# A binary convolution layer: own input buffers for even and odd rows, sign passes ordered behind the chunks, and y added to unscaled rows

## The chip, the cores and the metric

The kernel runs on one core of a Trainium2 chip. The metric is the device time of one launch in microseconds; the time of a kernel is the median of several runs. Engines are named as in the profile: PE (TensorE, matrix multiplication), PEld (its weight loads), DVE (VectorE), ACT (ScalarE), POOL (GpSimd) and SP (SyncE). SP only issues transfers here, POOL issues those that add to what lies in memory, and ACT issues a few stores.

## The reference

The network has four residual layers on a float32 tensor of 4 images, 256 channels, 64 x 64 pixels: an axial attention, a ternary convolution, a binary convolution and a convolution with generated weights. Each computes x = x + layer(group norm of x). The change concerns the third, cut to its computation:

```python
def _L2_conv_ref(x, w1, w2, g1, b1, g2, b2, g3, b3):
    x = channel_shuffle(x, 2)
    xa, xb = jnp.split(x, 2, axis=1)
    x1 = jnp.sign(x)
    x1 = gconv3x3(x1, w1, stride=1, groups=2)
    x1 = leaky_relu(x1)                              # slope 0.01
    x2 = batchnorm_train(x1, g1, b1)
    x3 = jnp.concatenate((x2 + xa, xb), axis=1)
    x3 = batchnorm_train(x3, g2, b2)
    x3 = channel_shuffle(x3, 2)
    x4 = jnp.sign(x3)
    x4 = gconv3x3(x4, w2, stride=1, groups=2)
    x4 = leaky_relu(x4)
    x4 = batchnorm_train(x4, g3, b3)
    x5a, x5b = jnp.split(x3, 2, axis=1)
    return jnp.concatenate((x4 + x5a, x5b), axis=1)
# in the network:  x = x + _L2_conv_ref(_gn(x), ...)
```

batchnorm_train takes mean and variance over the batch and all pixels, so the second convolution cannot start before the first has run on all four images.

## The kernel before

The attention and the ternary layer come first, then the binary layer (from 1884 to 2224 us of the trace), then the last layer, whose names begin with g. A tile scheduler orders each engine's instructions at compile time and sets the semaphore waits; each engine then works through its list in order. `tc.issue_after(ins)` puts what is traced inside it behind `ins` in the list of that instruction's engine, and adds no semaphore; `tc.high_priority()` moves work forward.

The channels of an image are kept as 128 even (t = 0) and 128 odd ones (t = 1), after the shuffle. "Even rows" and "odd rows" are these. The image is cut into halves h of 32 pixel lines, loaded with one more line (33 x 64 = 2112 elements in each of 128 partitions, 1056 KB, line 1704). A half is two chunks q. In `binary_conv` a chunk is 72 bf16 matmuls (L1613): 18 into each of four PSUM tiles m0 to m3, of which there are seven buffers. It works on transformed rows: `binary_rows` makes four combinations (e_tr, L1602, DVE) of the signs in a padded tile (e_pad), and each pair of image lines then costs four products rather than six. The chunk is emptied by an ACT copy of m1 (L1621), four DVE additions (L1622 to L1625), two DVE steps with the leaky slope that write y and its sums (L1628), and an ACT Square that sums y squared (L1631).

Pass 1 (`prepare_1`, `chunk_1`): for each half and t the rows are loaded (SP), ACT takes the sign of the rows less their group mean (L1726), and DVE transforms. For odd rows ACT then also writes scale times row plus bias over the rows (L1719), and POOL adds them to the output in memory (`into_out`, L1712). The cross sum of y and the even rows (L1739) gives, with the sums, the statistics of y + xa. The next image's half is prepared in the program's text after chunks 1 and 3 of the current one (`images`). The five row buffers are taken in turn, three in pool xp3 and one each in xp1 and xp2, whatever the rows are. What frees a buffer is for even rows the sign and the cross sums, and for odd rows the landing of the accumulating transfer.

Between the passes a chain of small DVE steps (L1796 to L1820 in the text) and two ACT calls gives the batch norm's factors: `sx`, `cx` per image for the rows, `sy1`, `cy1` for y, and `sa`, their product.

Pass 2 (`prepare_2`, `chunk_2`): the odd rows are loaded again, and ACT's sign with scale and bias is taken in two groups of 64 partitions (L1831). The even rows are loaded, scaled by ACT in place over all 2112 elements (L1847), y times `sa` is added by DVE (L1851), and then comes the plain sign in two groups (L1831). DVE transforms, and POOL adds the finished even rows to the output. Two entries in `ahead` keep the halves in order. The first half of image 0 is prepared in two steps of 17 and 16 lines. After chunks 1 and 3, ACT issues a store of y (L1870).

The last layer is traced after it. Its early steps share engines with pass 2: loads of finished output rows (`fetch`, SP), two measuring passes on ACT (L1267, L1268) placed behind chunks (2,1) and (2,2), a small norm, memsets of its padded tile (L1231), which uses memory that held y, and its first transforms (L1073 to L1095) and matmuls (L1113).

Of the kernel before, what the change touches and what calls it, by code (L numbers as in the profile page):

```python
# [9 lines left out]
F32 = mybir.dt.float32  # L10
F32R = mybir.dt.float32r
BF16 = mybir.dt.bfloat16
AF = mybir.ActivationFunctionType
ALU = mybir.AluOpType
# [4 lines left out]
P = 128  # L19
B = 4  # L20
# [21 lines left out]
def network(ctx: ExitStack, tc, x, wqkv, relm, relt, relw, relv, counts, masks, vecs, rowv, ab, w1, l2w1, l2w2, l3w, mats, out):  # L42
# [4 lines left out]
    nc = tc.nc  # L47
# [3 lines left out]
    keep = ctx.enter_context(tc.tile_pool(name="keep", bufs=1))  # L51
# [46 lines left out]
    def small(pool, shape, base="sm"):  # L98
        name = fresh(base)
        return pool.tile(shape, F32, name=name, tag=name)  # L100
# [65 lines left out]
    with ExitStack() as ph:  # L166
        wp = pool(ph, "a_w")
        xp_ = pool(ph, "a_x", 6)
        sp = pool(ph, "a_s")
# [5 lines left out]
        psp = pool(ph, "a_ps", 2, PSUM)  # L175
# [37 lines left out]
        squares = []  # L213
# [554 lines left out]
    def from_scores(general, keep):  # L768
# [836 lines left out]
        def binary_conv(psp, lp, parts, vs, q, dst, sums, squares, name):  # L1605

            ms = []
            for k in range(4):
                m = psp.tile([P, 8, 64], F32, name=f"{name}_{k}", tag="conv")
                for i in range(3):  # L1610
                    for dx in range(3):
                        for g in range(2):
                            nc.tensor.matmul(  # L1613
                                m[64 * g : 64 * g + 64], lhsT=parts[:, g, i, k, dx, :],
                                rhs=vs[g][:, k, 8 * (q % 2) : 8 * (q % 2) + 8, dx : dx + 64],
                                start=(i == 0 and dx == 0), stop=(i == 2 and dx == 2), tile_position=(0, 64 * g),
                            )
                ms.append(m)
            o = lp.tile([P, 2, 8, 64], F32, name=f"{name}_o", tag="lk")
            t, c = o[:, 0], o[:, 1]  # L1620
            nc.scalar.copy(c, ms[1])  # L1621
            nc.vector.tensor_tensor(t, ms[2], c, ALU.add)  # L1622
            nc.vector.tensor_tensor(c, c, ms[2], ALU.subtract)
            nc.vector.tensor_tensor(t, ms[0], t, ALU.add)
            nc.vector.tensor_tensor(c, c, ms[3], ALU.subtract)  # L1625
            rows = dst.rearrange("p (q r w) -> p r q w", r=2, w=64)
            for r in range(2):
                nc.vector.scalar_tensor_tensor(  # L1628
                    rows[:, r], o[:, r], 0.01, o[:, r], ALU.mult, ALU.max, accum_out=sums[:, r : r + 1]
                )  # L1630
            return nc.scalar.activation(o.rearrange("p r q w -> p (r q w)"), dst, AF.Square, accum_out=squares).ins  # L1631

        with ExitStack() as ph:
# [51 lines left out]
            def inside(t, h, rows=slice(0, P)):  # L1685
                return pads[t][h][rows, 1 - h : 34 - h, 1:65]
# [7 lines left out]
                binary_rows(v, pads[t][h])  # L1694
                return v

            taken = [0]

            def rows_of(b, t, h, name):

                xt = (xp3, xp3, xp3, xp1, xp2)[taken[0] % 5].tile([P, 33, 64], F32, name=f"{name}_{b}_{t}_{h}", tag="x2")
                taken[0] += 1
                r = 31 * h
                nc.sync.dma_start(
                    out=xt.rearrange("p h w -> p (h w)"), in_=x2_d[b][bass.ts(t, P), r * 64 : (r + 33) * 64]
                )
                return xt

            xa, xb = {}, {}

            def into_out(b, h, odd, xt):
                nc.gpsimd.dma_start(  # L1712
                    out=out[b].rearrange("(p two) f -> two p f", two=2)[odd][:, bass.ts(h, HW // 2)],
                    in_=xt.rearrange("p h w -> p (h w)")[:, 64 * h : 64 * h + HW // 2], accum_op=ALU.add,
                )

            def add_odd(b, h):
                own = xb[b, h][:, h : h + 32]
                nc.scalar.activation(own, own, AF.Identity, bias=cx[:, 1, b : b + 1], scale=sx[:, 1, b : b + 1])  # L1719
                into_out(b, h, 1, xb[b, h])  # L1720

            def prepare_1(b, h):
                vs = []
                for t in range(2):
                    xt = rows_of(b, t, h, "x2")
                    nc.scalar.activation(inside(t, h), xt, AF.Sign, bias=ngm2[:, b, t : t + 1])  # L1726
                    vs.append(transformed(b, t, h, 0))
                    (xa, xb)[t][b, h] = xt
                if b > 0:
                    add_odd(b, h)  # L1730
                return vs

            def chunk_1(b, q, vs):
                dst = y[b][:, bass.ts(q, 1024)]
                binary_conv(psp, lp, parts[0], vs, q, dst, sums[0][:, b, q], squares[0][:, b, q : q + 1], f"pc1_{b}_{q}")
                h = q // 2
                r = 16 * (q % 2) + h
                junk = jp.tile([P, 1024], BF16, name=f"junk_{b}_{q}", tag="junk")
                nc.vector.scalar_tensor_tensor(  # L1739
                    junk, dst, 1.0, xa[b, h][:, r : r + 16, :].rearrange("p h w -> p (h w)"), ALU.mult, ALU.mult,  # L1740
                    accum_out=cross[:, b, q : q + 1],
                )
# [34 lines left out]
            def half_scales(t, shift):  # L1777
                sz, cz = bn_affine(
                    sp, mean[:, t : t + 1], var[:, t : t + 1], vec[:, V_G2 + t : V_G2 + t + 1],
                    vec[:, V_B2 + t : V_B2 + t + 1], 1,  # L1780
                )
                if shift is not None:
                    nc.vector.scalar_tensor_tensor(cz, shift, sz, cz, ALU.mult, ALU.add)
                nc.vector.tensor_scalar(sx[:, t], rs2[:, :, t], sz, None, ALU.mult)
                nc.vector.tensor_scalar(cx[:, t], nmr2[:, :, t], sz, cz, ALU.mult, ALU.add)
                return sz

            half_scales(1, None)
            for h in range(2):
                add_odd(0, h)  # L1790
            images(prepare_1, chunk_1, ready)
# [9 lines left out]
            w = small(sp, [P, B])  # L1801
            nc.vector.scalar_tensor_tensor(w, my, 1.0 / HW, nmr2[:, :, 0], ALU.mult, ALU.mult)
            nc.vector.tensor_tensor(e, e, w, ALU.add)
            cov = small(sp, [P, 1])
            nc.vector.tensor_reduce(cov, e, AX.X, ALU.add)
            w = small(sp, [P, 1])
# [5 lines left out]
            nc.vector.scalar_tensor_tensor(var[:, 0:1], w, sy1, var[:, 0:1], ALU.mult, ALU.add)  # L1812
            nc.vector.tensor_scalar(var[:, 0:1], var[:, 0:1], 0.0, None, ALU.max)
            nc.vector.tensor_tensor(mean[:, 0:1], mean[:, 0:1], vec[:, V_B1 : V_B1 + 1], ALU.add)
            sa = small(sp, [P, 1])
            nc.vector.tensor_tensor(sa, sy1, half_scales(0, cy1), ALU.mult)

# [1 line left out]

            def prepare_2(b, h):
                xts = [rows_of(b, t, h, "x3") for t in range(2)]

                def signs(t, rows):
                    for g in range(2):
                        kw = {} if t == 0 else {
                            "bias": cx[64 * g : 64 * g + 64, 1, b : b + 1],
                            "scale": sx[64 * g : 64 * g + 64, 1, b : b + 1],
                        }  # L1830
                        sign = nc.scalar.activation(  # L1831
                            inside(g, h, slice(64 * t, 64 * t + 64))[:, rows], xts[t][64 * g : 64 * g + 64, rows],
                            AF.Sign, **kw,
                        )
                    return sign

                signs(1, slice(0, 33))
                vs = [slot(b, g, h, 1) for g in range(2)]

                steps = ((0, 17, 0), (17, 33, 8)) if b == h == 0 else ((0, 33, 0),)  # L1840
                n = 16 // len(steps)
                with ExitStack() as order:
                    for i in ahead:
                        order.enter_context(tc.issue_after(i))
                    for r0, r1, pair in steps:
                        xt = xts[0][:, r0:r1]
                        nc.scalar.activation(  # L1847
                            xt, xt, AF.Identity, bias=cx[:, 0, b : b + 1], scale=sx[:, 0, b : b + 1]
                        )
                        xf = xt.rearrange("p h w -> p (h w)")  # L1850
                        nc.vector.scalar_tensor_tensor(  # L1851
                            xf, y[b][:, 64 * (31 * h + r0) : 64 * (31 * h + r1)], sa, xf, ALU.mult, ALU.add
                        )
                        sign = signs(0, slice(r0, r1))
                        for g in range(2):
                            row = binary_rows(vs[g], pads[g][h], pair, n)
                ahead[:] = [sign.ins, row.ins]
                into_out(b, h, 0, xts[0])
                return vs

            ends = {}

            def chunk_2(b, q, vs):
                ends[b, q] = binary_conv(
# [162 lines left out]
```

## Time and profile before

| what | value |
|---|---|
| time, median of 3 runs | 2702.37 us (2691.62 to 2704.37) |
| the profiled execution's own time | 2695.66 us |
| its span in the trace | 2693.9 us |
| granted PE clock, mean | 0.94 |
| binary layer in the trace | about 1884 to 2224 us |
| PE busy in its 2304 matmuls | 273.7 us |
| ACT's wait for rows at the pass-1 signs | 54.9 us in 8 waits |
| PE idle between the passes | 17.66 us |

A group line of the profile reads: line, engine, operation, output and input names with buffer numbers left out, shapes, count; then busy time in us and the mean of one in ns; then the engine's idle time just before these instructions, with what ended most of it. A wait line reads: engine, tile and line that waited, what it waited for, us in total, times (in the binary layer's answer also the longest). A timeline line has the start, the duration, and the instruction; idle time before it stands in brackets. A stage line has, for each engine, busy time and instructions, and then the PE clock, the DMA share and GB/s.

### The profile page before, as it was taken

What the parts mean: (1) busy time and instruction counts of PE and PEld (TensorE: products, weight loads), DVE (VectorE), ACT (ScalarE), POOL (GpSimd) and SP (SyncE); (2) the same over time, 40 slices, a digit from 0 to 9 for tenths busy, and PEclk for the clock granted to TensorE, in tenths of its full rate; (3) what the DMA queues carried; (4) which work ended last, traced back from release to release, by engine and by line L of the source; (5) the groups of instructions that cost most, each with busy time, mean ns of one, the idle gap of its engine ahead of it and who ended that gap; (6) DMA issues with size and microseconds to landing.
All of it is one profiled execution on the core that took longest, in us unless ns stands there. A gap on an engine that the chain in (4) does not pass through costs nothing. (4 is left out here: it accounts for less than half of the span.)

```text
span 2693.9 us, 78726 instructions
## 1 busy us (share of the span) xinstructions
PE 2323.6 (86%) x34816; PEld 1620.9 (60%) x34816; DVE 1977.6 (73%) x3326; ACT 1299.7 (48%) x2114; POOL 167.8 (6%) x285
## 2 busy tenths in 40 slices
PE   7999888888998788878884999998887887899998
PEld 4656655556666566667663777776444444566665
DVE  6766787888876466666667989986677787688884
ACT  3556354555555654454434655553445753433210
POOL 0000100000000100000000011111000010100000
PEclk9999899999999789989896999999988997999999
DMA  6866476667666887777777666525655775746221
GB/s 234 269 194 196 127 196 183 169 155 202 177 156 146 251 276 252 255 245 257 249 237 255 225 206 226 181 110 193 160 152 170 237 263 150 160 108 148 42 47 49
DMA packets 284832, 505.64 MB, mean 188 GB/s; under 512 B 32896, under 2 KB 149248, under 8 KB 270784
## 3 DMA queue, kind: packets, MB, share of 16 engines
q1 hardware_dynamic: 214336, 347.46, 42.3%
q0 software_dynamic: 21888, 94.32, 13.8%
q10 hardware_dynamic: 48256, 58.73, 6.2%
q8 instruction: 275, 4.51, 0.7%
q14 instruction: 77, 0.63, 0.1%
HBM read 270.45 MB, written 229.97 MB: 186 GB/s over the span
## 5 line engine op out<-in xcount | busy, mean ns | idle before, releaser
L515 DVE STREAM_TRANSPOSE t<-pd 128x1024 f32<-128x1024 f32 x256 | 304.4, 1227 | 84.0 <-PE pd L508 83.1
L508 PE MATMUL pd<-rm,qb 64*32 64x256 f32 x8192 | 310.7, 390 | 48.8 <-DVE t L515 34.6
L1613 PE MATMUL pc<-e_tr,e_k 128*64 128x512 bf16 x2304 | 273.7, 399 | 59.5 <-DVE e_tr L1602 27.9
L535 ACT ACTIVATE o<-pq 128x512 f32<-128x512 f32 x256 | 150.5, 593 | 280.6 <-PE pq L529 280.6
L1113 PE MATMUL gc<-gtr,g_u 128*128 128x512 f32 x576 | 262.6, 608 | 12.8 <-DVE gtr L1077 5.4
L1613 PEld LDWEIGHTS <-e_k 128*64 128x64 bf16 x2304 | 155.6, 114 | 175.6 <-issue 73.9
L508 PEld LDWEIGHTS pd<-rm,qb 64*32 64x32 f32 x8192 | 171.5, 108 | 143.9 <-DVE t L515 60.5
L1509 PE MATMUL dc<-dh,d_u 128*128 128x512 f32 x768 | 230.9, 412 | 23.8 <-ACT dh L1486 21.1
L940 ACT ACTIVATE pt<-pt,sm 128x512 f32<-128x512 f32 x256 | 162.3, 709 | 167.6 <-DVE pt L910 167.6
L1509 PE MATMUL dc<-dl,d_u 128*128 128x512 f32 x768 | 226.5, 405 | 0.9 <-DVE dl L1487 0.7
L1113 PEld LDWEIGHTS gc<-gtr,g_u 128*128 128x128 f32 x576 | 111.2, 195 | 139.2 <-issue 121.3
L529 PEld LDWEIGHTS pq<-t,t 64*64 64x64 f32 x8192 | 143.8, 136 | 83.9 <-issue 74.7
L529 PE MATMUL pq<-t,t 64*64 64x64 f32 x8192 | 165.4, 224 | 26.9 <-issue 25.4
L1120 PE MATMUL gc<-gtc,g_u 128*128 128x256 f32 x768 | 177.5, 388 | 11.3 <-DVE gc_s L1140 7.3
L1509 PEld LDWEIGHTS dc<-dh,d_u 128*128 128x128 f32 x768 | 147.3, 193 | 64.5 <-ACT dh L1486 22.6
L1120 PEld LDWEIGHTS gc<-gtc,g_u 128*128 128x128 f32 x768 | 148.6, 194 | 49.3 <-issue 13.7
L1509 PEld LDWEIGHTS dc<-dl,d_u 128*128 128x128 f32 x768 | 144.8, 190 | 41.9 <-DVE dl L1487 3.4
L910 DVE TENSOR_TENSOR pt<-e_False,si_False 128x1024 f32<-128x1024 f32 x123 | 145.6, 1214 | 25.8 <-PE e_False L898 22.2
L898 PE MATMUL e_False<-qc_False,rw 32*128 32x256 f32 x984 | 124.1, 462 | 31.8 <-DVE pt L910 15.5
L541 ACT ACTIVATE sq<-o 128x1024 bf16<-128x1024 f32 x128 | 135.3, 1057 | 3.9
L291 PE MATMUL po<-xg,wt 128*128 128x512 f32 x256 | 121.0, 612 | 5.3 <-DVE st L298 3.7
L1003 PE MATMUL pe_False<-pt,ve 128*32 128x64 f32 x4096 | 90.8, 243 | 37.9 <-issue 33.1
(415 smaller groups left out, 3913.3 us busy)
## 6 DMA issues: line engine op xcount, KB each, us to landing
si_False<-qk_d SPq DMA_DIRECT2D x64, 1024.0 KB
qk_d<-o SPq DMA_DIRECT2D x496, 128.0 KB
x<-x_d SPq DMA_DIRECT2D x32, 1056.0 KB
gr<-out SPq DMA_DIRECT2D x16, 1056.0 KB
xa<-in_x SPq DMA_DIRECT2D x16, 1024.0 KB
vt_d<-vs ACTq DMA_DIRECT2D x32, 512.0 KB
q_d<-qs SPq DMA_DIRECT2D x64, 256.0 KB
qb<-q_d SPq DMA_DIRECT2D x128, 128.0 KB
```

The costliest lines, as they stand in the source:

```text
L508: nc.tensor.matmul(pds[t][32 * c : 32 * c + 32, m].rearrange("p j k -> p (j k)"), lhsT=q[rows, 2 * (gp % 2) + g, a, 32 * nb : 32 * nb + 32 ...
L515: nc.vector.transpose(ts[t][:, :, 32 * jh : 32 * jh + 32].rearrange("p a j b -> p j a b"), pds[t].rearrange("p m j k -> p j m k"),)
L529: nc.tensor.matmul(ps[nb][64 * g : 64 * g + 64, m, :], lhsT=ts[1][rows, n // 2, :, n % 2], rhs=ts[0][rows, n // 2, :, n % 2], start=True, ...
L535: nc.scalar.activation(o[:, :, n : n + 8, :], ps[nb].rearrange("p n (a b) -> p a n b", b=2), AF.Copy, accum_out=acc[:, nb, gp, col : col + 1],
L541: nc.scalar.activation(junk, part, AF.Square, accum_out=acc[:, 2, gp, col : col + 1])
L898: nc.tensor.matmul(rows_of_e[x_][:, :, :, par], lhsT=rw[rows, 63 - i : 127 - i].rearrange("p j r -> p (j r)"), rhs=q[rows, :, par, k % 2, ...
L910: nc.vector.tensor_tensor(dst, e, src, ALU.add)
L940: nc.scalar.activation(s, s, AF.Exp, scale=s2q[:, gp : gp + 1])
L1113: nc.tensor.matmul(ms[i], lhsT=u1[:, dx, k // 2, bass.ts(co, P)], rhs=v1[:, k // 2, :, dx : dx + 64], start=(first and dx == 0), stop=(las ...
L1120: nc.tensor.matmul(m[:, a], lhsT=u2[:, c, k // 2, bass.ts(co, P)], rhs=v2[:, c, k // 2].rearrange("p q w -> p (q w)"), start=first and a = ...
L1509: nc.tensor.matmul(at[k], lhsT=u[t][:, dx, k, bass.ts(co, P)], rhs=v[:, k, :, dx : dx + 64], start=(first and p_ == 0 and dx == 0), stop=( ...
L1613: nc.tensor.matmul(m[64 * g : 64 * g + 64], lhsT=parts[:, g, i, k, dx, :], rhs=vs[g][:, k, 8 * (q % 2) : 8 * (q % 2) + 8, dx : dx + 64], s ...
```

## The change

Three things are changed, all in the binary layer.

1. `rows_of` gives even rows to the three buffers of xp3 and odd rows to xp1 (first half) and xp2 (second half).
2. The signs are ordered on ACT behind the Square of given chunks. In pass 1 the sign of rows (b, h, t) follows the Square of chunk (b-1, 2h+t). In pass 2 the odd rows' signs of (b, h) follow the Square of chunk (b-1, 2h), the even rows' group that of (b-1, 2h+1); for image 0 the odd rows' signs follow pass 1's chunk (3, 1+h).
3. In pass 2, y times a new factor `ry` (y's scale times the standard deviation of the even rows' group, `ir2`) is added to the unscaled rows. The sign of even rows then carries scale and bias as that of odd rows did, and the scaling pass, over the 2048 elements of the half itself, comes after it, ahead of the accumulating transfer (`scaled_into_out`).

```diff
             def rows_of(b, t, h, name):
-                xt = (xp3, xp3, xp3, xp1, xp2)[taken[0] % 5].tile([P, 33, 64], F32, name=f"{name}_{b}_{t}_{h}", tag="x2")
-                taken[0] += 1
+                xt = (xp3, (xp1, xp2)[h])[t].tile([P, 33, 64], F32, name=f"{name}_{b}_{t}_{h}", tag="x2")
...
+            def scaled_into_out(b, h, odd, xt):
+                own = xt[:, h : h + 32]
+                nc.scalar.activation(own, own, AF.Identity, bias=cx[:, odd, b : b + 1], scale=sx[:, odd, b : b + 1])
+                into_out(b, h, odd, xt)
+
             def add_odd(b, h):
-                own = xb[b, h][:, h : h + 32]
-                nc.scalar.activation(own, own, AF.Identity, bias=cx[:, 1, b : b + 1], scale=sx[:, 1, b : b + 1])
-                into_out(b, h, 1, xb[b, h])
+                scaled_into_out(b, h, 1, xb[b, h])
...
                 for t in range(2):
                     xt = rows_of(b, t, h, "x2")
-                    nc.scalar.activation(inside(t, h), xt, AF.Sign, bias=ngm2[:, b, t : t + 1])
+                    with ExitStack() as order:
+                        if b > 0:
+                            order.enter_context(tc.issue_after(ends1[b - 1, 2 * h + t]))
+                        nc.scalar.activation(inside(t, h), xt, AF.Sign, bias=ngm2[:, b, t : t + 1])
...
+            ir2 = small(keep, [P, B])
+            nc.vector.reciprocal(ir2, rs2[:, :, 0])
...
+            ry = small(keep, [P, B])
+            nc.vector.tensor_scalar(ry, ir2, sy1, None, ALU.mult)
...
-            sa = small(sp, [P, 1])
-            nc.vector.tensor_tensor(sa, sy1, half_scales(0, cy1), ALU.mult)
+            half_scales(0, cy1)
...
                 def signs(t, rows):
                     for g in range(2):
-                        kw = {} if t == 0 else {
-                            "bias": cx[64 * g : 64 * g + 64, 1, b : b + 1],
-                            "scale": sx[64 * g : 64 * g + 64, 1, b : b + 1],
-                        }
+                        own = slice(64 * g, 64 * g + 64)
                         sign = nc.scalar.activation(
-                            inside(g, h, slice(64 * t, 64 * t + 64))[:, rows], xts[t][64 * g : 64 * g + 64, rows],
-                            AF.Sign, **kw,
+                            inside(g, h, slice(64 * t, 64 * t + 64))[:, rows], xts[t][own, rows],
+                            AF.Sign, bias=cx[own, t, b : b + 1], scale=sx[own, t, b : b + 1],
                         )
...
-                signs(1, slice(0, 33))
+                with tc.issue_after(ends[b - 1, 2 * h] if b > 0 else ends1[B - 1, 1 + h]):
+                    signs(1, slice(0, 33))
...
+                    if b > 0:
+                        order.enter_context(tc.issue_after(ends[b - 1, 2 * h + 1]))
                     for r0, r1, pair in steps:
                         xt = xts[0][:, r0:r1]
-                        nc.scalar.activation(
-                            xt, xt, AF.Identity, bias=cx[:, 0, b : b + 1], scale=sx[:, 0, b : b + 1]
-                        )
                         xf = xt.rearrange("p h w -> p (h w)")
                         nc.vector.scalar_tensor_tensor(
-                            xf, y[b][:, 64 * (31 * h + r0) : 64 * (31 * h + r1)], sa, xf, ALU.mult, ALU.add
+                            xf, y[b][:, 64 * (31 * h + r0) : 64 * (31 * h + r1)], ry[:, b : b + 1], xf, ALU.mult, ALU.add
                         )
...
-                into_out(b, h, 0, xts[0])
+                scaled_into_out(b, h, 0, xts[0])
```

`chunk_1` now keeps what `binary_conv` returns, its Square, in `ends1[b, q]`; the dictionary `ends` for pass 2 is created earlier. The lines below the first edit move by a few: the sign of pass 1 becomes L1730, the cross sum L1745, the signs of pass 2 L1837, the addition of y L1857, and the scaling pass of both passes L1717.

More of the change, by code (lines that the diff above doesn't have):

```diff
@@ L1695, in transformed @@
                 return v
-            taken = [0]
             def rows_of(b, t, h, name):
-                xt = (xp3, xp3, xp3, xp1, xp2)[taken[0] % 5].tile([P, 33, 64], F32, name=f"{name}_{b}_{t}_{h}", tag="x2")
-                taken[0] += 1
+                xt = (xp3, (xp1, xp2)[h])[t].tile([P, 33, 64], F32, name=f"{name}_{b}_{t}_{h}", tag="x2")
                 r = 31 * h
@@ L1709, in from_scores @@
             xa, xb = {}, {}
+            ends1, ends = {}, {}
             def into_out(b, h, odd, xt):
@@ L1734, in chunk_1 @@
                 dst = y[b][:, bass.ts(q, 1024)]
-                binary_conv(psp, lp, parts[0], vs, q, dst, sums[0][:, b, q], squares[0][:, b, q : q + 1], f"pc1_{b}_{q}")
+                ends1[b, q] = binary_conv(
+                    psp, lp, parts[0], vs, q, dst, sums[0][:, b, q], squares[0][:, b, q : q + 1], f"pc1_{b}_{q}"
+                )
                 h = q // 2
@@ L1857, in prepare_2 @@
                 ahead[:] = [sign.ins, row.ins]
-                into_out(b, h, 0, xts[0])
+                scaled_into_out(b, h, 0, xts[0])
                 return vs
-            ends = {}
             def chunk_2(b, q, vs):
```

## The prediction

> **What bounds the kernel now.** I read the page's first and fifth parts, then for the binary layer alone (1884 to 2224 us of the trace) the waits, the groups by line, and the table by stage.
>
> ```profile
> span 2693.9 us, 78726 instructions
> PE 2323.6 (86%) x34816; PEld 1620.9 (60%) x34816; DVE 1977.6 (73%) x3326; ACT 1299.7 (48%) x2114; POOL 167.8 (6%) x285
> ...
> L1613 PE MATMUL pc<-e_tr,e_k 128*64 128x512 bf16 x2304 | 273.7, 399 | 59.5 <-DVE e_tr L1602 27.9
> ```
>
> PE is busy 86% of the span, but in this layer it is short of work: its 2304 matmuls come at 108 ns, 7.8 us for each of 32 chunks (72 matmuls), 249 us in 340. The layer's share is what the change can move: 91 us.
>
> ```profile
> ACT e_pad L1726 <- DMA x<-x_d: 54.9, 8, 12.1
> DVE pc_o L1622 <- ACT pc_o L1621: 46.0, 13, 10.3
> PE pc L1613 <- DVE e_tr L1602: 27.9, 3, 17.7
> PE pc L1613 <- ACT pc_o L1621: 26.1, 11, 7.9
> ```
>
> The waits (total, times, longest) say why. ACT stands 54.9 us in front of pass 1's signs (L1726) for rows that haven't landed. The copies (L1621) that empty PSUM stand behind those signs on the same in-order engine, DVE's evacuation (L1622) waits 46.0 us for the copies, and PE for both. The timeline shows one such case:
>
> ```profile
> 2010.34 2.06 ACT L1726 ACTIVATE e_pad<-x,sm 128x2112 bf16<-128x2112 f32 x1 [10.40 <-DMA x<-x_d]
> 2012.30 1.04 ACT L1631 ACTIVATE pc_o<-y 128x1024 f32<-128x1024 f32 x1
> ...
> 2013.34 2.08 ACT L1719 ACTIVATE x<-x,sm,sm 128x2048 f32<-128x2048 f32 x1
> 2015.33 0.56 ACT L1621 COPY pc_o<-pc 128x512 f32<-128x512 f32 x1
> ```
>
> Pass 2 is different: by stages (PE, PEld, DVE, ACT, POOL busy, clock, DMA share, GB/s) ACT is the limit in its first 80 us, with 31.5 of 40 us.
>
> ```profile
> 2064.00:2104.00 40.00, 36.02 (x290) 21.91 (x292) 30.21 (x54) 31.54 (x23) 1.70 (x2) 0.89 0.89 244
> 2184.00:2224.00 40.00, 35.59 (x307) 19.24 (x304) 34.15 (x80) 15.01 (x22) 4.30 (x6) 0.99 0.74 274
> ```
>
> By the starts of L1622, the first eight chunks of pass 2 come every 11.6 us, while ACT prepares up to two images ahead, and the last seven every 7.5, at PE's pace, with nothing left to prepare.
>
> **Durations used**, all from the layer's groups:
>
> ```profile
> L1602 DVE TENSOR_TENSOR e_tr<-e_pad 128x1056 bf16<-128x1056 bf16 x107 | 69.3, 701 | 28.7 <-ACT e_pad L1726 17.3 <-ACT e_pad L1831 11.4
> L1831 ACT ACTIVATE e_pad<-x,sm,sm 64x2112 bf16<-64x2112 f32 x16 | 34.4, 2147 | 21.5 <-DMA x<-x_d 17.1 <-DVE x L1851 4.1
> L1831 ACT ACTIVATE e_pad<-x 64x2112 bf16<-64x2112 f32 x14 | 27.5, 1966 | 2.6 <-DVE x L1851 2.4
> L1726 ACT ACTIVATE e_pad<-x,sm 128x2112 bf16<-128x2112 f32 x12 | 24.6, 2057 | 56.4 <-DMA x<-x_d 54.9 <-DVE sm L1755 1.4
> ...
> L1851 DVE SCALAR_TENSOR_TENSOR x<-y,sm,x 128x2112 f32<-128x2112 f32 x7 | 16.9, 2412 | 2.2 <-ACT x L1847 2.2
> L1719 ACT ACTIVATE x<-x,sm,sm 128x2048 f32<-128x2048 f32 x8 | 16.6, 2086 | 0.8 <-DVE sm L1785 0.8
> ```
>
> Back to back, e_tr comes every 0.62 us (2.5 for four) and L1851 costs 2.22 where it stands between two of DVE's steps. From a chunk's L1622 to its Square (L1631) are 3.86 us, the Square takes 1.18 with its read, a copy 0.61. A chunk without preparation is therefore .61+3.86+1.18 = 5.65 us of chain, under PE's 7.8.
>
> **Part 1: own buffers, and the pin in pass 1.** In the compiled order each image-b sign now stands right behind the Square of chunk (b-1, 2h+t), so one per chunk, and the scale pass (L1719) behind the next copy, in the shadow of DVE's evacuation (2.08 of 3.86 us). Even rows rotate over three buffers that nothing but pass 1's cross sum (L1739) has to release: no out accumulation (8.6 us to landing) and no queueing behind one. Odd rows still wait for theirs, but two chunk pairs (some 36 us) ahead of need.
> What replaces the load wait is a chain of pinned steps. First chunk of a pair: 3.86 + 1.18 + sign 2.08 + copy .61 = 7.73 to the second's L1622. There one e_tr stands inside the evacuation: .62 + 3.86 + 1.18 + 2.08 + four e_tr 2.5 = 10.2 to the next. A pair takes 17.9 us, 8.95 a chunk, 15% above PE's floor. Times by L1622's start, before then after: chunk (1,0) 1938.4 / 1933.8 (first loads unchanged, one wait for a load left); two images of two pairs: (3,0) 2021.8 / 2005.4; the last image, where pins end, 26.7 / 23.7. Pass 1 gives **-19.4 us**.
> This holds if an even load lands within the 8.9 us from the last cross of a pair (6.3 us after L1622) to the sign that needs it (10.2 + 3.86 + 1.18 after it). The trace's load issued at 2002.66 was used at 2010.34: 7.7 us beside other transfers. The Trainium skill ("DMA: Bandwidth & Descriptors", section "Anatomy of one DMA") [...]says that a semaphore is waited for at the issuing sequencer. [...]by the row 1.2, and with an out accumulation beside it perhaps none. I take the row: no stall, bounds 0 and +3 us at each of five loads.
>
> **Part 2: y on unscaled rows, between the passes.** Before, from the end of the last cross (2053.75) the statistics run to 2058.4, then L1847 in halves, L1851, and the first sign at 2063.10; PE at 2064.82, +11.07. Now two halves of L1851 (2.54 us) stand in the statistics chain on DVE, the scale is folded into the sign (half size about 1.27 with operands, 1.11 without), and L1847 leaves the path: sign at 4.7 + 2.54 = +7.3, PE at about +9.1. **-1.9 us**.
>
> **Part 3: pass 2.** ACT's sums hardly change: per half image, two signs grow by .18 each, and the scale pass shrinks from 2.15 to 2.09. L1847 no longer stands ahead of L1851 and sign; as the new scale pass it stands behind a copy. The out accumulation then waits for ACT, not DVE; it lands with a whole image to spare. What changes is where four signs stand. They may not run two images ahead in ACT's idle time; they are pinned one image ahead, so preparation goes on through chunk (2,3), 12 chunks rather than 8. A pair's chain: evacuation with L1851 inside 3.86 + 2.22, Square 1.18, sign 2.17, copy .61 = 10.0; then 3.86 + 1.18 + two signs 4.34 + the last one's four e_tr 2.5 + hand-overs .3 = 12.2 (the fourth sign runs behind a copy, under the evacuation). 22.2 us a pair, 11.1 a chunk.
> - Image 0 carries 46.8 instead of 46.6 from its first L1622 to the next image's: +.2. Image 1: 44.4 for 46.2: -1.8.
> - Image 2 was free of preparation and took 30.3; it will take 44.4: **+14.1**.
> - What is queued behind moved work: DVE's memset of the next layer's pad (L1231) uses y1's room, and waits for both stores of y1, the second issued when chunk (1,3) ends. It used to come after L1622 of (2,0) and waited .2 us; now it stands right behind (1,3)'s evacuation and ahead of eight e_tr. The store took 8.0 us (issued 2159.86, released 2167.92), e_tr could otherwise start at 3.4 and finish by 8.4; with the stall 13.4: **+5.0** (bounds 0, +8), as (2,0)'s L1622 is behind them.
> - The next layer's measuring passes (L1267 and L1268, 1.9 us each), which ran in ACT's idle time, are now between Square (2,1) and the signs: **+4.0**; the second pair, with the norm's L106, stands in (2,3) and is partly covered: **+2.9**.
> - Image 3 at PE's pace again, with the next layer's first transforms: +.8.
>
> Sum for pass 2 with the start: -1.9 + .2 - 1.8 + 14.1 + 5.0 + 6.9 + .8 = **+23.3**. The next layer then starts as it did, 3.8 us after its last wait; its g_y load, which now follows image 3's accumulation, lands (about +184 after pass 1's end) before it is wanted (+195).
>
> **PE's clock.** PE will now idle 6.6 us of each pair in pass 2. In the trace 72 matmuls after a gap of 4.20 us took 10.47 us, after 1.92 us 8.04. The skill ("TensorE: Matmul & The Clock Gate", Part 1) has the clock at half after about 3.4 us of idle, for about as long. By the rule single gaps of 3.3 stay just short of it: 0. By the row with 4.20, should gaps join, a chunk costs 10.5: still under 11.1, also 0 in the sum, except in chunks at PE's pace after (3,0): +2.4. I take 0.
>
> **Sum.** 2695.7 (the profiled execution) - 19.4 + 23.3 = 2699.6. The shown median is 6.7 above the profiled one, so **2706** beside 2702.4: no difference that can be told, since 0.5% (13.5 us) is about what a measurement of this kernel can tell from no change.
>
> **Rivals.**
> - *Even loads too late* (slower): pass 1's chain is refilled by loads with 1.2 us of slack. From 10.6 us a load on (5 to 6 loads), each us over costs 5 to 6; at 12 us, the longest wait seen, +16: 2722. For: DMA share .70 in pass 1, odd and even loads issued together. Against: 7.7 us seen. A fifth.
> - *Pass 2 stretches further* (slower): the stores of y1 and measured rows come later still (+8 and a second wait), or the next layer's opening slips: 2720. One tenth.
> - *The chain isn't the limit in pass 2* (faster): hand-overs overlap, so a pair runs at 18.4 rather than 22.2 over six pairs, -23: 2683. For: chunks in image 3 ran at 7.5. Against: these had no signs, and both engines are in order. With a smaller form of it (no stall at L1231, -5, and pass 1 at PE's floor, -9): 0.15.
> - *As summed*: 0.55.
>
> Range 2688 to 2724: from the lesser fast case to the late loads, each far end left out. Chances: faster .15, same .55, slower .30.
>
> **What would show it.** Right: ACT's wait for x at the pass-1 signs falls from 54.9 to under 15; L1622 every 17.9 us a pair; pass 1 ends near 2034; between passes PE idles some 2 us less; image 2 of pass 2 takes over 50 us; L1231 waits 5 to 8 us for y_d. Wrong: DMA still tops ACT's waits in pass 1, or pass 2's pairs run under 20 us, or the layer ends more than 14 us from 2227.

## The result and the profile after

The changed kernel takes 2708.51 us (median of 20 runs, 2697.30 to 2723.83), the kernel before in its 20 runs 2701.05 (2686.48 to 2717.76). The ratio is 1.0032 with a 95% interval of 1.0012 to 1.0053: 0.3% slower, inside the 0.5% that was called no difference, and near the forecast of 2706 against 2702.4. This near-zero is two large things that cancel: pass 1 and the gap gain 23.6 us, pass 2 and the tail lose 26.3.

All stages below are read from L1622, the first evacuation step of a chunk, in the profiled execution of each kernel. "Pass 1" and "pass 2" run from the first to the sixteenth L1622 of a pass, "gap" from the last of pass 1 to the first of pass 2, "layer" from the binary layer's first matmul to the last layer's first, and "tail" from the last L1622 to the end of the span. A row without a ratio rests on a single run. Where a pin is named, it is an `issue_after` of the change's second part; chunk (b, q) is chunk q of image b.

| kernel | pass 1 | gap | pass 2 | layer | tail | ratio to before (95%) |
|---|---|---|---|---|---|---|
| before | 156.1 | 25.8 | 145.5 | 338.3 | 474.1 | |
| changed | 135.5 | 22.7 | 167.5 | 337.6 | 478.4 | 1.0032 (1.0012 to 1.0053) |
| changed, again | 135.2 | 22.5 | 167.8 | 337.8 | 479.5 | single run |
| 1 buffers alone | 133.7 | 23.1 | 141.4 | 309.1 | 468.3 | 0.9879 (0.9844 to 0.9914) |
| 2 buffers, pass 1's pins | 138.8 | 23.0 | 141.0 | 314.1 | 470.3 | 0.9878 (0.9840 to 0.9917) |
| 3 changed, pass 2 unpinned | 138.7 | 23.1 | 134.2 | 307.1 | 473.7 | 0.9901 (0.9865 to 0.9936) |
| 4 y on unscaled rows alone | 155.5 | 25.8 | 152.1 | 344.3 | 471.8 | 1.0044 (1.0023 to 1.0066) |
| 5 pass 1's pins alone | 137.1 | 25.8 | 145.8 | 321.5 | 472.0 | single run |
| 6 changed, no pins | 132.9 | 22.6 | 134.7 | 301.6 | 470.6 | 0.9864 (0.9841 to 0.9887) |
| 7 changed, memsets later | 135.3 | 23.1 | 164.2 | 334.5 | 479.5 | 1.0010 (0.9980 to 1.0039) |
| 8 changed, measuring later | 135.3 | 23.1 | 164.4 | 336.4 | 475.0 | single run |
| 9 changed, odd pin alone in pass 2 | 135.3 | 24.1 | 146.5 | 317.3 | 475.6 | single run |
| 10 changed, even pin alone in pass 2 | 140.9 | 23.7 | 155.4 | 331.9 | 478.4 | single run |
| 11 changed, pins for image 1 of pass 1 alone | 141.4 | 23.4 | 134.4 | 310.4 | 471.1 | 0.9902 (0.9863 to 0.9940) |

The page of the changed kernel (same parts as before):

```profile
span 2716.4 us, 78715 instructions
PE 2334.4 (86%) x34816; PEld 1610.1 (59%) x34816; DVE 1977.6 (73%) x3327; ACT 1301.2 (48%) x2113; POOL 167.9 (6%) x285
...
L1613 PE MATMUL pc<-e_tr,e_k 128*64 128x512 bf16 x2304 | 273.5, 398 | 54.8 <-DVE pc_o L1623 28.0
```

This execution is 22.5 us longer in span than the profiled one of before, but 20.1 of them lie ahead of the binary layer, which began at 1904.2 us here and at 1884.1 there. In the repeat of the same kernel it began at 1890.4, and in the 14 traces of this study anywhere from 1882.7 to 1904.2. The comparison that counts is by stage.

PE's wait in the layer fell by only 4.7 us, and has another name: not the copies, but L1623, by which DVE releases PSUM. The waits of the changed kernel from 1884 to 2234 us (total, times, longest):

```profile
ACT pc_o L1631 <- DVE y L1628: 115.1, 28, 9.6
...
DVE pc_o L1622 <- ACT pc_o L1621: 30.0, 10, 4.9
PE pc L1613 <- DVE pc_o L1623: 28.0, 11, 7.1
...
PE pc L1613 <- DVE e_tr L1602: 20.1, 1, 20.1
...
PE pc L1613 <- ACT pc_o L1621: 6.8, 5, 3.2
```

The 54.9 us in which ACT stood for rows at pass 1's signs have become 4.7, in one wait. In their place ACT now stands 115.1 us for DVE's y (61.9 before, and 122.8 when the last chunks, up to 2242 us, are counted as well): it reaches a Square, may not take a pinned sign ahead of it, and waits.

```profile
L1730 ACT ACTIVATE e_pad<-x,sm 128x2112 bf16<-128x2112 f32 x12 | 24.5, 2045 | 4.7 <-DMA x<-x_d 4.7
```

By stages (columns as before) the start of pass 2 leaves ACT room, 27.0 of 40 us for 31.5. The second line holds the evacuations of chunk (1,3) and of the first two chunks of image 2. There ACT falls from 31.7 us (in the 40 us from 2144 of the trace before) to 23.2, and every engine is thin: PE is busy 31.3 us, at a clock of 0.83. Image 2 by itself, 2164.9 to 2215.9, has a clock of 0.84, and ACT is busy in 35.8 of its 51.0 us.

```profile
2062.00:2102.00 40.00, 36.69 (x304) 21.70 (x306) 33.43 (x59) 27.03 (x20) 2.55 (x3) 0.93 0.73 186
2142.00:2182.00 40.00, 31.25 (x242) 15.29 (x244) 22.15 (x44) 23.20 (x21) 0.84 (x1) 0.83 0.62 180
```

### The profile page after: what moved, and what is told of

Read it like the earlier page. It is cut to its first block, busy times and chain, and to the rows that moved or that the text cites. A ratio compares the mean times of both kernels' runs of the same rounds, so it can differ in the third digit from the quotient of the medians.

```text
span 2716.4 us, 78715 instructions
## 1 busy us (share of the span) xinstructions
PE 2334.4 (86%) x34816; PEld 1610.1 (59%) x34816; DVE 1977.6 (73%) x3327; ACT 1301.2 (48%) x2113; POOL 167.9 (6%) x285
## 5 line engine op out<-in xcount | busy, mean ns | idle before, releaser
L1613 PEld LDWEIGHTS <-e_k 128*64 128x64 bf16 x2304 | 140.0, 114 | 186.5 <-issue 48.7
L529 PEld LDWEIGHTS pq<-t,t 64*64 64x64 f32 x8192 | 146.5, 138 | 88.5 <-issue 77.3
L1120 PE MATMUL gc<-gtc,g_u 128*128 128x256 f32 x768 | 175.5, 384 | 14.4 <-DVE gc_s L1140 10.3
L1509 PEld LDWEIGHTS dc<-dh,d_u 128*128 128x128 f32 x768 | 147.3, 193 | 64.6 <-ACT dh L1486 22.6
L910 DVE TENSOR_TENSOR pt<-e_False,si_False 128x1024 f32<-128x1024 f32 x123 | 145.7, 1215 | 24.3 <-PE e_False L898 23.6
L541 ACT ACTIVATE sq<-o 128x1024 bf16<-128x1024 f32 x128 | 135.3, 1057 | 3.9
```

The costliest lines, as they stand in the source:

```text
L529: nc.tensor.matmul(ps[nb][64 * g : 64 * g + 64, m, :], lhsT=ts[1][rows, n // 2, :, n % 2], rhs=ts[0][rows, n // 2, :, n % 2], start=True, ...
L541: nc.scalar.activation(junk, part, AF.Square, accum_out=acc[:, 2, gp, col : col + 1])
L910: nc.vector.tensor_tensor(dst, e, src, ALU.add)
L1120: nc.tensor.matmul(m[:, a], lhsT=u2[:, c, k // 2, bass.ts(co, P)], rhs=v2[:, c, k // 2].rearrange("p q w -> p (q w)"), start=first and a = ...
L1509: nc.tensor.matmul(at[k], lhsT=u[t][:, dx, k, bass.ts(co, P)], rhs=v[:, k, :, dx : dx + 64], start=(first and p_ == 0 and dx == 0), stop=( ...
L1613: nc.tensor.matmul(m[64 * g : 64 * g + 64], lhsT=parts[:, g, i, k, dx, :], rhs=vs[g][:, k, 8 * (q % 2) : 8 * (q % 2) + 8, dx : dx + 64], s ...
```

## The experiments

**1 and 2: buffers alone, and with pass 1's pins.** My theory was that pass 1 gains by both together, and that what pass 2 loses comes from its pins. Experiment 1 is the first hunk of the change and nothing else:

```diff
-                xt = (xp3, xp3, xp3, xp1, xp2)[taken[0] % 5].tile(...)
-                taken[0] += 1
+                xt = (xp3, (xp1, xp2)[h])[t].tile(...)
```

> The kernel before with the buffer assignment alone (even rows in the three buffers, odd rows in one for each half), no pins, the old scaling in pass 2. Theory (a late load in front of a copy is what pass 1 loses, and both the buffers and the order decide it): even rows are freed earlier, but the list of ScalarE still takes odd signs one image ahead of their chunk, whose buffer waits for an out accumulation, so part of the gain: ScalarE's wait for rows at pass 1's signs falls from 54.9 us to 20 to 40, time ratio 0.994 to 1.0. Rival (the buffers alone are the gain, the pins only stretch the chain): wait under 10 us and ratio 0.992 or less.

Experiment 2 adds to it the `issue_after(ends1[b - 1, 2 * h + t])` of pass 1's signs, and leaves pass 2 as it was.

> Buffers and pass 1's pins, pass 2 as in the kernel before. Theory: the whole of pass 1's gain without pass 2's loss: pass 1 ends about 20 us earlier than before after its start, pass 2 takes 145 us between its first and last evacuation as before, the next layer's weights are loaded some 45 us ahead as before; ratio 0.9925 (0.991 to 0.995). Rival (the earlier end of pass 1 is given back in pass 2 because loads and accumulations crowd together): ratio 0.998 or more.

Measured: the buffers alone bring pass 1 from 156.1 to 133.7, the gap from 25.8 to 23.1, pass 2 from 145.5 to 141.4, the layer from 338.3 to 309.1, and the ratio to 0.9879, beyond what I expected. The waits of the kernel with the buffers alone still show rows awaited at pass 1's signs, 28.6 us for 54.9, as expected:

```profile
ACT e_pad L1723 <- DMA x<-x_d: 28.6, 5, 9.0
```

So the wait and the time don't go together: half the wait is left, and all of the time is gained, because of where the remaining waits stand: 16.8 us of them fall in the first image, where the kernel before has 19.9, and after the other three (11.8 us) PE idles only 2.2. With the pins added the wait falls to 4.3 us and pass 1 is 5.1 us longer. Of that, 3.3 us is not the pins' own chain. In experiment 2 the first odd signs of pass 2, which no pin holds, stand inside pass 1 and wait there for their rows, 5.7 us of it in chunk (2,3):

```profile
ACT e_pad L1834 <- DMA x<-x_d: 8.2, 2, 5.7
```

The step from (2,3) to (3,0) takes 15.5 us there and 10.0 in the changed kernel, whose pin on pass 2's odd rows keeps these signs out; all of pass 1 is 135.5 us there for 138.8. The first experiment's expectation fell in its time, not in its wait. The second one's theory held for pass 2 (141.0 us for 145), and its ratio was better than its range.

**5: the pins alone.** If the buffers are the gain, pins without them should bring nothing.

```diff
+                    with ExitStack() as order:
+                        if b > 0:
+                            order.enter_context(tc.issue_after(ends1[b - 1, 2 * h + t]))
-                    nc.scalar.activation(inside(t, h), xt, AF.Sign, ...)
+                        nc.scalar.activation(inside(t, h), xt, AF.Sign, ...)
```

> The kernel before with pass 1's pins alone; five buffers taken in turn, no pins in pass 2, old scaling. Theory (the gain is the buffers', which free the loads; the pins add none): loads still wait for buffers that an accumulation holds, and ScalarE still waits over 30 us for rows at pass 1's signs: pass 1 takes 145 to 165 us from first to last evacuation (before 156.1), the binary layer 330 to 345 us from its first matmul to the next layer's (before 338.3). Rival (the order in ScalarE's list is what costs): pass 1 under 142 us, layer under 325.

Measured: pass 1 takes 137.1 us, the layer 321.5, so the theory fell and the rival held. Waits of this kernel at pass 1's signs:

```profile
ACT e_pad L1730 <- DMA x<-x_d: 15.4, 4, 5.9
```

The pins alone gain 19.0 us of pass 1, the buffers alone 22.4, both together 17.3 (experiment 2), and 20.6 with pass 2's pins. They are two cures of one ill. Before, ACT's list had signs up to two chunks ahead of where the pins put them, at places where their rows hadn't landed; from 1900 to 2060 us SP stood 100.1 us in eight waits for accumulations, with the loads behind them. Either the rows come sooner or the sign is asked for later. The traces show both. The load for pass 1's last sign goes out after 8 of its chunks in experiment 1, after 11 before. In experiment 5 it goes out after 10, but the sign comes 21 us behind it rather than 7. Experiment 1 doesn't part the two altogether, since the scheduler makes ACT's list anew for other buffers. Once one cure is there the other adds nothing, and the pins' own chain costs.

**3, 4 and 6: the unscaled addition and pass 2's pins.** Experiment 3 takes both pins out of `prepare_2` (and leaves `ahead`, which was there before). Experiment 4 is the kernel before with the unscaled addition alone. Experiment 6 is the changed kernel without any pin.

```diff
-                with tc.issue_after(ends[b - 1, 2 * h] if b > 0 else ends1[B - 1, 1 + h]):
-                    signs(1, slice(0, 33))
+                signs(1, slice(0, 33))
...
-                    if b > 0:
-                        order.enter_context(tc.issue_after(ends[b - 1, 2 * h + 1]))
```

> The changed kernel without the pins of pass 2; y still added to unscaled rows. Theory (the pins, by stretching preparation to chunk (2,3), cost pass 2 its 22 us and the late weight load 4): all of that comes back: pass 2 takes 145 us between first and last evacuation, the first matmul of the last layer waits under 4 us, ratio to the kernel before 0.991 (0.989 to 0.994). Rival (the order on DVE and ScalarE that the unscaled addition brings is itself slower): pass 2 over 155 us, ratio 0.996 or more.

> The kernel before with only the addition of y to unscaled rows (old buffers, no pins). Theory: 2 to 3 us between the passes, nothing in pass 1, pass 2 within 3 us: ratio 0.999 (0.996 to 1.001). Rival (the signs with scale and bias, and the scaling pass behind them, load ScalarE in the first 80 us of pass 2, which it bounds): pass 2 longer by 5 us or more, ratio 1.002.

> The changed kernel without any pin: own buffers, y on unscaled rows. Theory (buffers give about -29 us, the unscaled addition with them another -7 in pass 2, pass 1's pins +5): binary layer 302 us, pass 1 134, pass 2 134; ratio to the kernel before 0.985 (0.981 to 0.989). Rival (the pins of pass 1 are needed once y is added to unscaled rows): pass 1 over 139 or layer over 307 us.

Measured: without pass 2's pins it takes 134.2 us rather than 167.5, so the pins cost it 33.3, more than the 22.0 by which it exceeds the kernel before. The rest was hidden by gains that I hadn't seen: buffers (145.5 to 141.4) and the addition on unscaled rows (141.0 to 134.2, experiment 2 against 3). In experiment 4 the same addition, with buffers taken in turn, makes pass 2 longer by 6.6 us, its rival's case. Waits at pass 2's signs there, from 2040 to 2250 us:

```profile
ACT e_pad L1838 <- DMA x<-x_d: 29.0, 5, 8.4
```

One of these, 4.8 us, still lies in pass 1; the other 24.2 us in four compare with 12.1 in two before. The out accumulation now follows the scaling pass behind the signs: the first of pass 2 goes out 3.4 us ahead of pass 2's first evacuation, 11.6 before, and the next load goes out 0.1 us after it has landed. With own buffers loads still wait for accumulations, but no sign of pass 2 stands for rows after its first evacuation (experiments 3 and 6). In experiment 2, with the addition of before, one did, for 7.5 us ahead of chunk (1,1), and PE then idled 9.2: this is about what the new addition gains there. Experiment 6 came out as expected, 301.6 us for the layer (302) and 0.9864 (0.985).

The gap tells against a step of mine. Timelines, with idle time before an instruction in brackets: first experiment 2 (old order of scale and addition), then experiment 3 (addition within the statistics).

```profile
2038.26 1.22 DVE L1742 SCALAR_TENSOR_TENSOR junk<-y,x 128x1024 bf16<-128x1024 f32 x1
...
2044.13 2.42 ACT L1850 ACTIVATE x<-x,sm,sm 128x1088 f32<-128x1088 f32 x2 [1.40 <-DVE sm L1788]
2045.46 2.55 DVE L1854 SCALAR_TENSOR_TENSOR x<-y,sm,x 128x1088 f32<-128x1088 f32 x2 [1.36 <-ACT x L1850]
2046.85 4.41 ACT L1834 ACTIVATE e_pad<-x 64x1088 bf16<-64x1088 f32 x4 [0.29 <-DVE x L1854]
...
2048.57 6.78 PE L1613 MATMUL pc<-e_tr,e_k 128*64 128x512 bf16 x41 [18.17 <-DVE e_tr L1602]
```

```profile
2043.50 1.22 DVE L1745 SCALAR_TENSOR_TENSOR junk<-y,x 128x1024 bf16<-128x1024 f32 x1
...
2047.03 2.54 DVE L1854 SCALAR_TENSOR_TENSOR x<-y,sm,x 128x1088 f32<-128x1088 f32 x2
2051.91 5.15 ACT L1837 ACTIVATE e_pad<-x,sm,sm 64x1088 bf16<-64x1088 f32 x4 [1.40 <-DVE sm L1791]
2053.24 5.59 DVE L1602 TENSOR_TENSOR e_tr<-e_pad 128x528 bf16<-128x528 bf16 x16 [1.36 <-ACT e_pad L1837]
2053.82 6.39 PE L1613 MATMUL pc<-e_tr,e_k 128*64 128x512 bf16 x37 [18.18 <-DVE e_tr L1602]
```

From the start of the last cross sum to the first matmul are 10.31 us and 10.32: the same. The addition costs the statistics what scale and addition in halves cost behind them. What shortened the gap was something else. In the kernel before, an odd sign of the second half stood between the scale and the first even sign, because its rows had come late (SP issued their load at 2053.86):

```profile
2060.92 2.15 ACT L1831 ACTIVATE e_pad<-x,sm,sm 64x2112 bf16<-64x2112 f32 x1
```

It is gone from there in every kernel with own buffers (gap 22.5 to 24.1; from the last cross sum to the first matmul 10.3 us), and still there in 4 and 5, which have 25.8 (12.7 and 12.2 us; before 12.2).

**7 and 8: what image 2 pays.** Experiment 7 puts the last layer's memsets behind DVE's last transform, experiment 8 its measuring passes one image later. All pins stay.

```diff
-            set_up(0)
+            with tc.issue_after(ahead[1]):
+                set_up(0)
```

```diff
-                    with tc.issue_after(ends[2, 1 + h]):
+                    with tc.issue_after(ends[3, h]):
                         measure(0, 1, h)
```

> The changed kernel, all pins kept, with the next layer's three small memsets (the one at L1231 waits for y's stores) put behind VectorE's last transform of the binary layer. Theory (the store's landing stalls VectorE 6.5 us ahead of eight transforms): chunk (1,3) to (2,0) falls from 15.3 to about 10 us, pass 2 from 167.5 to about 162, ratio to the kernel before 1.001 (0.998 to 1.003). Rival (ScalarE's chain hides the stall, or the wait comes back at the next instruction that needs y's room): pass 2 stays over 166.

> The changed kernel, all pins kept, with the next layer's measuring passes ordered behind chunks (3,0) and (3,1) rather than (2,1) and (2,2). Theory (they lengthen ScalarE's chain by 4.0 and 2.9 us in image 2): (2,1) to (2,2) falls from 16.0 to about 12 us and (2,3) to (3,0) from 15.4 to about 12.5, pass 2 from 167.5 to about 161; the next layer's first matmul may be later, as its factors are (5 to 15 us after the last evacuation, 3.8 now). Rival (they run in ScalarE's idle time): both intervals stay within 1 us.

Measured: the changed kernel's timeline on DVE, and the store on ACT's queue, show the stall that was forecast. The wait is put down to a copy, which had ended 0.6 us earlier. In the kernel before, the same memset is released by the store of y (first line). Here the store was issued 6.4 us ahead of the memset; its landing isn't listed, and that it came last is inferred.

```profile
2167.92 0.11 DVE L1231 MEMSET g_pad<- 128x66 f32 x1 [0.22 <-DMA y_d<-y]
...
2153.25 0.08 DVE L1628 DVE_READ_ACCUMULATOR y<-pc_o 128x1 f32 x1
2159.81 0.11 DVE L1231 MEMSET g_pad<- 128x66 f32 x1 [6.48 <-ACT pc_o L1621]
...
2160.51 4.41 DVE L1602 TENSOR_TENSOR e_tr<-e_pad 128x1056 bf16<-128x1056 bf16 x7
```

```profile
2153.37 0.33 ACTq L1874 DMA_DIRECT2D y_d<-y  x1
```

With the memsets moved, chunk (1,3) to (2,0) takes 12.1 us rather than 15.3, so the stall cost 3.3, not some 5 as expected; 12.05 is what that step takes in images 0 and 1, and I had set it at 10. Pass 2 falls by 3.3 to 164.2. The time ratio of 1.0010 agrees, but its interval overlaps that of the changed kernel. With measuring later, (2,1) to (2,2) falls from 16.0 to 12.1, and (2,3) to (3,0) from 15.5 to 12.1: 3.9 and 3.4 for 4.0 and 2.9. Image 2 as a whole gains 6.9, since (2,2) to (2,3) grows by 0.4. Image 3 then carries 3.6 of it, so that pass 2 takes 164.4 us and not 161.

**9 and 10: one pin of the two.** Experiment 9 keeps the odd rows' pin of pass 2 and drops the even rows'; experiment 10 the other way round.

> The changed kernel with the even rows' pin of pass 2 taken out and the odd rows' pin kept. Theory (a half's transforms need both kinds of signs, so either pin alone keeps preparation going through chunk (2,3)): pass 2 takes 155 to 168 us. Rival (the even rows' pin, which also holds the addition's consumers and the out accumulation, carries the loss): pass 2 140 us or less.

> The changed kernel with the odd rows' pin of pass 2 taken out and the even rows' pin kept. Theory, as for the other pin: 155 to 168 us for pass 2. Rival (the odd sign between Square and the next copy carries the loss): 140 us or less.

Measured: 146.5 and 155.4 us, against 134.2 without and 167.5 with both. The odd pin costs 12.3, the even pin 21.2, together 33.5 for 33.3 seen. Neither theory nor rival of experiment 9 had this middle; experiment 10 is at the lower edge of the theory. That either pin alone would keep all of the loss is refuted: in pass 2 the costs add. The odd pin gives some of its cost back in pass 1, as it keeps pass 2's first signs out of it (138.7 to 135.3 us from experiment 3 to 9, 140.9 to 135.5 from 10 to the changed kernel). In the whole layer it costs 10.2 us, the even pin 24.8, both 30.5.

**The changed kernel again, and pins for image 1 alone.** Experiment 11 is number 6 with `if b == 1:` around pass 1's pin.

> The changed kernel once more, unedited. Theory (the layers before the binary one vary from execution to execution and the change has no part in it; the late weights are the change's): the binary layer's first matmul comes anywhere between 1884 and 1905 us, while pass 1 (135.5), the gap (22.7) and pass 2 (167.5) repeat within 0.5 us, and the last layer's first matmul again waits 7 to 9 us for its weights. Rival (the changed kernel slows the earlier layers): first matmul again at 1900 or later.

> Own buffers, y on unscaled rows, no pins in pass 2, and in pass 1 pins for image 1 only. Theory (the pins shorten pass 1's first image from 48.7 to 41.4 us because there the first loads are late, and the free order is faster afterwards, 34.5 us an image for 35.2, and 17.8 for 24 at the end): pass 1 126 to 130 us, binary layer 295 to 299, ratio to the kernel before 0.984 (0.980 to 0.988). Rival (what the first image gains comes back as later loads): pass 1 132 or more, ratio as without pins, 0.986.

Measured: the repeat has the three stages within 0.4 us and began the layer at 1890.4, 13.8 us earlier with the same kernel, so the late start of the first execution needs no cause in the change. The last layer's first matmul again waited for its weights, 6.8 us. Experiment 11 missed: pass 1 takes 141.4 us, ratio 0.9902. The first image is shorter at its start (chunk (0,2) at 23.7 us for 25.0), and then the rival's case holds: later loads. ACT stands 33.3 us for rows at pass 1's signs, 27.6 without pins, four of the waits in images 1 and 2, and pass 1 is 8.5 us longer than in number 6. By its layer number 6 is the best of these kernels, and 1.4% faster than before; its ratio alone can't be told from those of 1 and 2.

## Why the prediction was right, step by step

- **Pass 1, -19.4:** measured -20.6, and by parts: (1,0) came at 41.4 us after the first evacuation (41.4 forecast), a pair took 17.6 (17.9), the last image 23.7 (23.7). The loads stayed within their slack, without a stall at the pins. Even rows of images 2 and 3 were issued 8.8 us ahead of their signs (8.9 forecast), and ACT waited for none of them; its one wait, of 4.7 us, was for an odd load of image 1, which took 8.8. How close it was, the trace before shows: where ACT waited for rows in pass 1, they took 5.0 to 11.4 us from issue to sign. (By its semaphore the sign at 2010.34 waited for the second of two loads, issued at 2003.03: 7.3 us, not 7.7.) The step's tacit claim that buffers and pins are both needed was wrong, as experiments 1 and 5 show.
- **Between the passes, -1.9:** counted as in the forecast, PE's first matmul came 9.2 us after the end of the last cross sum, 11.07 before: -1.9, and -3.0 from L1622 to L1622. This was luck, as the cause was wrong. Moving the addition is worth 0.0 (10.31 and 10.32 us). The forecast put the whole path before down to scale and addition, and overlooked the odd sign of 2.15 us in it; that it left is the gain. The sign that PE would idle some 2 us less failed: it idles 20.1 us, 17.7 before. The odd signs pinned behind chunks (3,1) and (3,2) hold up the evacuation of pass 1's last chunks, so PE is done 9.8 us ahead of the last cross sum rather than 5.4.
- **Pass 2, images 0 and 1:** 46.9 us (46.8) and, with the memset's stall, 47.5 (49.4). A pair took 22.1 us (22.2). The chain that I added up from ACT's and DVE's durations is what set the pace.
- **L1231, +5.0:** +3.3. The stall came, and the size was off; that the store took 6.4 us, for 8.0 in the trace before, is about the difference.
- **Measuring passes, +6.9:** 6.9 in image 2, by experiment 8.
- **Image 2 in all:** 51.1 us where 51.3 was forecast. **Image 3, +.8:** -.3.
- **"The next layer then starts as it did":** this step failed. By the order of the pools the first of its weights take the room of padded sign tiles, which the prolonged preparation frees later. POOL issued the first of these loads 44.8 us ahead of the last evacuation before, and 23.7 ahead after the change; three of the later ones then waited in line. PE's timeline:

```profile
2241.79 4.07 PE L1113 MATMUL gc<-gtr,g_u 128*128 128x512 f32 x4 [8.54 <-DMA g_u<-u_d]
...
2265.69 0.59 PE L115 MATMUL pst<-sm,mt 128*128 128x1 f32 x2 [11.62 <-DVE sm L1276]
```

and POOL's:

```profile
2214.26 0.56 POOL L1239 DMA_DIRECT2D g_u<-uc_d  x1 [22.50 <-ACT pc_o L1621]
...
2230.52 0.76 POOL L1241 DMA_DIRECT2D g_u<-u_d  x1 [8.58 <-DMA out<-x]
```

  The first line waited 3.75 us before, the second 8.44. The late weights by themselves are little: the first of these matmuls comes 3.8 us after the last evacuation, 2.7 before. The larger loss is at rows of the output that DVE needs for the second line (wait lines of before and after):

```profile
DVE gr L1306 <- DMA gr<-out: 7.3, 1, 7.3
...
DVE gr L1306 <- DMA gr<-out: 11.7, 1, 11.7
```

  SP issued them 0.8 us later than before, counted from the last evacuation, and they were there 5.2 us later. In the 20.2 us after that evacuation the DMA engines are now busy all the time (share 1.01 by the records, 394 GB/s, for 0.61 and 219), since the last weights land 24 us after it, 4 before. Six kernels keep a pin in pass 2, and have tails of 475.0 to 479.5 us; the eight that don't have 468.3 to 474.1. On average that is 6 us. That the weights crowd out these rows is read from the traces; no run tested it by itself.
- **PE's clock:** PE's longest wait for L1623 was 7.1 us, not 3.3, and the granted clock 0.84 in image 2. Single waits of 3.8 and 3.5 us in image 1 came with 0.84 as well (2117.4 to 2149.5), one of 3.1 in image 0 with 0.96. As forecast it cost the sum nothing that shows, since image 2 came out at 51.1: PE wasn't what it waited for.

Sum by the traces: -20.6 - 3.0 + 22.0 + 4.3 (tail) = +2.7 us from the layer's first evacuation, against +3.9 forecast. So near a sum is in part luck: up to the last evacuation the kernel did 5.5 us better than forecast (pass 1 by 1.2, the gap by 1.1, pass 2 by 3.2), and the tail, put at nothing, took 4.3 of it back. The 20 runs a side say +8.6 (0.32% of 2701), with an interval of +3.2 to +14.3; one trace a side can't tell more.

The rivals: late loads didn't happen. The fast case asked for a chain in pass 2 that isn't the limit; with the pins it was. But pass 2 without pins at 134.2 us shows how much lay in that direction, had the change not carried them.

## What to carry to other kernels

When a change has several parts, price each alone against the kernel before, and also what it adds once the others are there: here two parts gained 22 and 19 us alone and 17 together, one part was worth -7 or +7 depending on another, and the last cost 33. An order pinned to a milestone turns an engine's slack into a chain (each step waits for the one before it on another engine); add that chain up, and compare it with the pace of the engine that it feeds, before pinning. And ask what else waits for the memory that a prolonged phase holds, stores and the next phase's weights included.

## What the runs showed of the hardware that was not expected

With unchanged code ahead of it, the binary layer began between 1882.7 and 1904.2 us in 14 traces, a spread of 21.5 us, and 13.8 us apart in two traces of one kernel, whose pass 1, gap and pass 2 repeated within 0.4 us. A change of a few microseconds in such a kernel is read from stages; from whole times it takes 20 runs a side to see 0.2%.
